# Output projections as seven half-block products in a planned attention kernel

## The chip, the core and the metric

The kernel runs on one core of one Trainium2 chip. The metric is the device time of one execution in microseconds, the median of several runs. The core has five engines that run side by side and wait for each other through semaphores: TensorE (PE: matmuls, with its weight loads as PEld), VectorE (DVE), ScalarE (ACT), GpSimd (POOL) and SyncE (SP), from whose queue nearly all transfers start. Each engine works through its own list of instructions in order.

## What is computed

One layer over 4096 rows of 512 numbers (x), with 3202 rows of context, all float32. In short form:

```python
def layer(x, context):                       # x: 4096 x 512, context: 3202 x 512
    q = heads(layernorm(x, g1, beta1) @ Wq.T + bq)          # 8 heads of 64
    k, v = (heads(layernorm(context, g1, beta1) @ W.T + b) for W, b in ((Wk, bk), (Wv, bv)))
    attn = softmax(q @ k.T / sqrt(64)) @ v
    x1 = x + attn.reshape(4096, 512) @ W_o.T + b_o          # the output projection
    u = (layernorm(x1, g2, beta2) @ W_in.T + b_in) @ Bmat   # 4096 x 64
    s = 0
    for t in range(4096):
        s = silu(s @ A.T) + u[t]
        out[t] = x1[t] + s @ Cmat
    return out + (program_probs.mean(0) @ W_prog.T + b_prog)
```

## The kernel before

**Stages.** A lead of some 186 us turns the context into keys and values and stores them in HBM. Then comes attention: 8 blocks of 512 query rows (`QB`), in each 4 pairs of heads and 2 halves of 256 rows (`QU`), which makes 64 units. A unit walks over the keys in 13 steps of 256. In each step TensorE makes a group of scores (L1095, 16 matmul instructions in 64x64 tiles of the array), ScalarE turns them to weights by an exponential (`weights`, L1172), VectorE adds the weights into the denominators (`add`, L1180), and TensorE multiplies them with the values (`product`, L1229, 16 instructions in 64x64 tiles). The weights live in a ring of `NP` = 15 tiles, from ScalarE's writing until VectorE and TensorE have read them. At the end a unit's output is copied, joined, divided by its denominators (`output`, `join`, `inverse`, `scale`) and kept as a tile of 128 x 256. The scan over the rows is solved by sweeps that mix with the last block and the end, which begins when the last attention product is done.

**Around the units.** Queries of the next block (`queries`): rows are loaded, normalised, turned (`flip` L441, `move` L453) and projected by `by_sevenths`: a product of two matrices, each cut in four quarters, is made from seven products of quarters in place of eight, with sums before and after. `seventh` (L364) is one such product: four matmuls of 128x128 weights by 256 columns. `CHAIN` is the order 1, 2, 6, 5, 7, 3, 4; two banks of PSUM, x and y, take turns, and a product that adds on to a bank waits until the product before it in that bank was read (`before`). Sums of the moving side are made on VectorE (L1468), reads on ScalarE (L1491) and VectorE (L1487).

Output projection (`project`): per half block of 256 rows, two tiles of 128 rows, each by four matmuls of 128x512 (`outs`, L1561); VectorE adds the residual (`x1_`, L1574), which GpSimd has prepared (`row`, L1555); then the second normalisation, `mod` (GpSimd, L1578), the store, the turn, and the product `inputs` (L1618) that gives the scan its input. Blocks 0 to 6 do this for both halves behind the block; of block 7 the first half goes this way and the second through `last_products` (L1881) in the end, beside the last denominators (L1244).

**The order.** `Plan` holds all pieces of the attention stage with engine, cost, dependencies, due date and the rings (`take`, `give`) that they occupy; `order()` runs an event queue over these costs and hands out, engine by engine, the ready piece with the earliest date. The result is the fixed order of instructions. A PE piece of another kind than the last one (64x64 tiles are "quarters", the full array has no kind) costs `ENTER` or `LEAVE` more; pieces of the full array are held together by `KEEP` and `ALONE`. `SHIFT` moves the dates of sorts of pieces by steps of 2150 ns. Loads of keys and values are no pieces: each group of scores issues those of 10 and 6 steps ahead (`load_k` L392, `load_v` L400) on SP's queue when its turn comes.

Of the kernel before, what the change touches and what calls it, by code (L numbers as in the profile page):

```python
# [20 lines left out]
P = 128  # L21
# [20 lines left out]
NP = 15  # L42
NA = 3
# [28 lines left out]
class Plan:  # L72
# [8 lines left out]
    ENTER, LEAVE = 110, 147  # L81
# [3 lines left out]
    PORT = ("add", "rest", "fold", "gather", "scale", "t", "tq", "tied", "wk", "wv", "wq", "rowv")  # L85

    SHIFT = {
        "row.store": 11.5, "fold": 2, "rows.outs": 0.75, "heads": -12, "sample": -3, "spread": 4.75,
        "query.flip": -11, "states": -5.5, "inverse": 4.75, "extra": 10, "scale": -57.75, "rest": -1,
        "row.mod": -17, "joined0": -14.25, "b": -15, "add.l": -23, "l.stats": -34.75, "last": -4.5,  # L90
        "base": -34.75, "inverse.l": -27, "rows.inputs": 3.5, "maximum": -13.5, "fall": -19, "query.stats": -8,
        "den": 4.5, "row.scaled": 12, "l.h": -7, "row.stats": -9.25,
    }

    def __init__(self, rings, held):
# [4 lines left out]
    def add(self, name, engine, cost, run, after=(), due=0, take=(), give=(), kind=None):  # L100
# [4 lines left out]
        elif sort in self.UNIT and name[1] >= self.ENDS:  # L105
# [4 lines left out]
            give=give, kind=kind, at=len(self.pieces),  # L110
# [4 lines left out]
    def order(self):  # L115
# [26 lines left out]
        while len(out) < len(pieces):  # L142
            for e in self.LATE:
# [24 lines left out]
                free[e] = now + cost  # L168
                if shares(p):
                    port = free[e]  # L170
                heapq.heappush(events, (free[e], 0, p["at"], p))
                heapq.heappush(events, (free[e] + self.LATE[e], 1, p["at"], p))
# [5 lines left out]
            while events and events[0][0] <= now:  # L178
                _, late, _, p = heapq.heappop(events)
                if late:  # L180
# [12 lines left out]
def xattn_ssm_kernel(  # L193
# [886 lines left out]

    def parts_of(t):
# [3 lines left out]
    o_t = {}  # L1085
# [194 lines left out]
    def finish(w, i, d, plan):  # L1280
# [33 lines left out]
        plan.add(("output", i), "ACT", 360, partial(output, w), [("product", i, NDC - 1)], d, ["o_"])  # L1314
# [6 lines left out]
        else:  # L1321
            plan.add(("fold", i), "DVE", 680, partial(fold, w), [("add", i, NDC - 1)], d + 500)
            plan.add(("swap", i), "ACT", 760, partial(swap, w), [("fold", i)], d + 600, ["rd"])
            plan.add(("gather", i), "DVE", 860, partial(gather, w), [("swap", i)], d + 700, [],
                     [("rd", ("swap", i))])
            plan.add(("sums", i), "PE", 300, partial(sums, w), [("gather", i), from_(d + 8 * STEP)], d + 1000,
                     ["m", "m"], acc, "quarters")
            opened = ("den", i, 0)
            for k in range(2):
                plan.add(("den", i, k), "ACT", 450, partial(denominators, k),  # L1330
# [19 lines left out]
    def norm_pieces(plan, ks, gets, d, after, names, gives, wait):  # L1350
# [21 lines left out]
        for t, (k, v) in enumerate(zip(ks, vs)):  # L1372
            plan.add((*k, "stats"), "DVE", 870, partial(stats_, v, gets[t], names[t]),
                     [after[t]] + ([(*ks[0], "stats")] if t else []),
# [7 lines left out]
    def queries(plan, Q, d):  # L1382

        copied, w = [], {}
        of_xn = ("query", Q, 0, "move0")
        for half in range(2):
# [4 lines left out]
            def load(t, v=v, at=at):  # L1391
                if t == 0:
                    v["x"] = xp_.tile([P, 2, H], F32, tag="x", name=f"x_{at[0]}")
# [21 lines left out]
            for t in range(2):  # L1415
                plan.add((*ks[t], "flip"), "DVE", 720,
# [7 lines left out]
            d += 2 * QSTEP  # L1424
# [4 lines left out]
    def query_weights(plan, after, d):  # L1429
# [11 lines left out]
        for i, (k, x, y, op) in enumerate(sums):  # L1441
            first = {"6": "5", "7": "6", "3": "7"}.get(k)
            plan.add(("sq", k), "POOL", 1300, partial(sum_, k, x, y, op),
                     [("sq", first)] if first else after, d + i * STEP)

# [6 lines left out]
    def by_sevenths(plan, Q, w, copied, d, of_xn):  # L1452
# [53 lines left out]
        for at, k in enumerate(CHAIN):  # L1506
# [7 lines left out]
            plan.add(("sevenths.read", Q, k), on, 950 if on == "ACT" else 690, partial(read, k), [(*key, k)], d + at, [], gives)  # L1514
# [23 lines left out]

    def project(plan, Q, halves, d, index):

        for half in halves:
# [3 lines left out]
            last = Q == NQB - 1  # L1545
            now = plan.ALONE if last else 0

            def load(t, vs=vs, w=w, at=at):
                if t == 0:
                    w["x"] = xp_.tile([P, 2, H], F32, tag="x", name=f"xr_{at[0]}")  # L1550
# [33 lines left out]
            for t in range(2):  # L1584
# [3 lines left out]
                         [(*ks[t], "load")] + ([] if last else [from_(d - 2 * STEP)]), d - STEP)  # L1588
            plan.add((*k2, "outs"), "PE", 7200, outs,
                     [("scale", i, 0) for i in units_] + [(*k, "row") for k in ks], d - now,  # L1590
                     ["m", "m", "x1"], [("o_", ("output", i)) for i in units_])
            for t in range(2):
# [4 lines left out]
                             [f"y{r}" for r in at], [("x1", (*k2, "outs"))] * 2 * last,  # L1597
                             [] if last else [from_(d + 18 * STEP)])
            for t in range(2):
                plan.add((*ks[t], "mod"), "POOL", 1280, partial(mod, vs[t]), [(*ks[t], "x1")], d + 2 * STEP,  # L1600
                         [], [("x1", (*k2, "outs"))] * last)
                plan.add((*ks[t], "store"), "SP", 800, partial(store, vs[t], at[t]),
                         [(*ks[t], "mod" if last else "flip")], d + 3 * STEP, [], [("x", (*ks[0], "load"))])
# [10 lines left out]
            def inputs(w=w, at=at, last=last):  # L1614
                w["pu"] = m_tile([P, P], f"pu_{at[0]}")
                for c in range(NC):
                    for t in range(2):
                        nc.tensor.matmul(  # L1618
                            w["pu"][t * NS : (t + 1) * NS], wc[:, c, :],
                            w["xn"][:, t, c, :] if last else mixed(w["xn"][:, c, :], t),  # L1620
# [3 lines left out]
            def kept(t, w=w, at=at):  # L1624
                to, c0 = divmod(at[t] // L, NCK)
                hs, of = slice(to * NS, (to + 1) * NS), slice(t * NS, (t + 1) * NS)
                nc.scalar.activation(
                    u[hs, :, c0 : c0 + P // L].rearrange("s j c -> s c j"),
                    w["pu"][of].rearrange("s (c j) -> s c j", j=L),
                    AF.Identity,  # L1630
                    bias=bu2[of],
                    scale=2.0,
                )

            if last:
                plan.add((*k2, "turn"), "PE", 1050, turn, [(*k, "scaled") for k in ks], d + 5 * STEP - now,
                         ["m", "m", "xn2"], [("xh", (*ks[0], "scaled"))])
                for t in range(2):
                    plan.add((*ks[t], "copy"), "ACT", 560, partial(copy, t),
                             [(*k2, "turn")] + ([(*ks[0], "copy")] if t else []), d + 6 * STEP + t, [],  # L1640
                             [("m", (*k2, "turn"))])
                copied, xn2, after = [(*k, "copy") for k in ks], (*k2, "turn"), 7
            else:
                copied, xn2, after = [], (*ks[0], "move0"), 16

                def move_(a, w=w, at=at):
                    if a == 0:
                        w["xn"] = xp_.tile([P, NC, QU], F32, tag="xn2", name=f"xn2_{at[0]}", bufs=1)
                    move(w["xn"], w["x1"], a)

                for t in range(2):
                    plan.add((*ks[t], "flip"), "DVE", 720, lambda t=t, w=w, nv=nv: flip(w["x1"], nv[t]["xh"], t),
                             [(*k, of) for k in ks for of in ("scaled", "mod")], d + 5 * STEP + t, [],
                             [("xh", (*ks[0], "scaled"))])
                for a in range(P // TB):
                    plan.add((*ks[0], f"move{a}"), "SP", 2600, partial(move_, a),
                             [(*k, "flip") for k in ks] + ([xn2] if a else []), d + (6 + 2 * a) * STEP,
                             [] if a else ["xn2"], [("x1", (*k2, "outs"))])
# [796 lines left out]
```

## Time and profile before

| | us |
|---|---|
| median of 3 runs | 1912.04 (1910.61 to 1912.35) |
| the profiled execution | 1913.58 |
| its span, first to last instruction | 1911.7 |
| mean granted TensorE clock | 0.998 |
| lead, up to the first scores of attention | some 186 |
| end, after the last attention product | 55.13 |

The profile is of one execution. It names engines PE, PEld, DVE, ACT, POOL and SP; L12 is line 12 of the kernel. A row of the timeline gives the start in us, the duration, the engine, the line and operation, what is written from what, and how many instructions it merges; in square brackets stands how long the engine was idle before it, and who released it. A row of a group gives "busy us, mean ns of one | idle time before, by releaser". A row of waits gives who waited for whom: the total in us, how often, the longest. A row of a stretch gives its length and the busy time and instructions of each engine. Matmul instructions are pipelined, so their durations overlap: what one costs is read from the distance of starts. A float32 matmul of the program is two matmul instructions.

### The profile page before, as it was taken

How to read it: one execution, taken by the hardware profiler on the slowest of the kernel's cores; microseconds unless marked ns; L12 is line 12 of the kernel's file. 1: busy time of each engine (PE TensorE's matmuls, PEld its weight loads, DVE VectorE, ACT ScalarE, POOL GpSimd, SP SyncE). 2: the span in 40 equal slices, each digit the busy share in tenths (PEclk: the TensorE clock that was granted, in tenths of full speed). 3: DMA queues.
4: the chain of work that ended last, by engine and by line, in shares of the span. 5: the costliest groups of instructions: out<-in, count | busy, mean ns of one | idle time of the engine just before them, and what ended most of it. 6: DMA issues, size and time to landing. Idle time of an engine off the chain costs nothing.

```text
span 1911.7 us, 68126 instructions
## 1 busy us (share of the span) xinstructions
PE 1895.2 (99%) x29464; PEld 1352.6 (71%) x29464; DVE 1535.3 (80%) x2084; ACT 1176.6 (62%) x1675; POOL 237.7 (12%) x382
## 2 busy tenths in 40 slices
PE   9999999999999999999999999999999999999997
PEld 5887679766677667766777667766776677766675
DVE  6642699788879889788878887888978887988876
ACT  3242677576666666656757665766756775756653
POOL 6120000001100120011000120012001110011105
PEclk9999999999999999999999999999999999999999
DMA  7554233132422343224413242234322341544577
GB/s 254 156 158 123 63 102 88 45 101 77 110 71 84 92 126 93 81 75 112 110 41 93 81 121 75 82 89 122 101 68 75 96 122 46 160 120 133 175 197 224
DMA packets 260764, 207.50 MB, mean 109 GB/s; under 512 B 94632, under 2 KB 233896, under 8 KB 260460
## 3 DMA queue, kind: packets, MB, share of 16 engines
q1 hardware_dynamic: 256440, 196.48, 36.6%
q10 hardware_dynamic: 4020, 6.62, 1.1%
q8 instruction: 233, 3.82, 0.9%
q14 instruction: 71, 0.58, 0.1%
HBM read 156.32 MB, written 29.88 MB: 97 GB/s over the span
## 4 chain that ended last, share of the span: by engine, by line


## 5 line engine op out<-in xcount | busy, mean ns | idle before, releaser
L1172 ACT ACTIVATE p<-s,shifts 128x1024 f32<-128x1024 f32 (+1 forms) x832 | 892.9, 1082 | 481.1 <-PE s L1095 464.0
L1180 DVE TENSOR_TENSOR acc<-p,acc 128x1024 f32<-128x1024 f32 (+1 forms) x704 | 829.1, 1178 | 119.8 <-ACT p L1172 85.9
L1095 PE MATMUL s<-q,k 64*64 64x256 f32 x12800 | 837.4, 377 | 0.2 <-ACT p L1172 0.2
L1229 PE MATMUL po<-p,v 64*64 64x256 f32 x12800 | 837.4, 377 | 0.0
L1095 PEld LDWEIGHTS s<-q,k 64*64 64x64 f32 x12800 | 499.9, 133 | 199.5 <-ACT p L1172 16.4
L1229 PEld LDWEIGHTS po<-p,v 64*64 64x64 f32 x12800 | 496.4, 133 | 177.1 <-issue 12.9
L1555 POOL TENSOR_TENSOR xr<-xr,rowb 128x512 f32<-128x512 f32 x30 | 41.3, 1390 | 994.3 <-DMA xr<-in_x_dram 467.4
L1301 DVE RECIPROCAL rd<-rd 128x256 f32<-128x256 f32 (+1 forms) x64 | 110.2, 1723 | 23.5 <-ACT rd L1296 23.5
L1561 PE MATMUL pa<-wo,o 128*128 128x512 f32 x240 | 107.0, 599 | 0.0
L1180 DVE TENSOR_TENSOR acc<-p,p 128x1024 f32<-128x1024 f32 x64 | 78.2, 1222 | 10.9 <-ACT p L1172 10.6
L1561 PEld LDWEIGHTS pa<-wo,o 128*128 128x128 f32 x240 | 44.4, 190 | 56.0 <-issue 56.0
L1204 DVE TENSOR_TENSOR acc<-swap,acc 64x256 f32<-64x256 f32 x126 | 56.7, 450 | 8.9 <-ACT swap L1199 7.0
L1166 DVE TENSOR_TENSOR acc<-x,acc 2x256 f32<-2x256 f32 x128 | 55.0, 430 | 2.5
L1199 ACT COPY swap<-acc 64x256 f32<-64x256 f32 x126 | 50.8, 403 | 6.5 <-DVE acc L1187 3.4
L1578 POOL TENSOR_TENSOR xr<-x,modb 128x512 f32<-128x512 f32 x30 | 38.2, 1273 | 116.9 <-DVE x L1574 116.9
L1491 ACT ACTIVATE q<-qx,bias 128x256 f32<-128x256 f32 x42 | 17.6, 471 | 45.8 <-PE qx L364 45.8
L542 DVE TENSOR_TENSOR ks<-pky,ks 128x512 f32<-128x512 f32 x15 | 10.4, 692 | 43.6 <-PE pky L364 28.7
L1362 POOL TENSOR_SCALAR rstd_x<-mv_x 128x1 f32<-128x1 f32 x28 | 6.2, 221 | 313.5 <-DVE mv_x L1359 311.8
L536 ACT ACTIVATE ks<-pkx,bias 128x256 f32<-128x256 f32 x40 | 16.8, 471 | 45.0 <-PE pkx L364 33.6
L1187 DVE TENSOR_TENSOR acc<-acc 128x512 f32<-128x512 f32 x63 | 43.2, 686 | 1.4
L1278 DVE TENSOR_TENSOR o<-po,o 128x256 f32<-128x256 f32 x64 | 27.0, 421 | 12.3 <-ACT o L1274 7.6
L1129 DVE TENSOR_REDUCE m<-sm 128x1 f32<-128x256 f32 x64 | 24.1, 419 | 15.7 <-PE sm L1115 15.2
(283 smaller groups left out, 1588.8 us busy)
## 6 DMA issues: line engine op xcount, KB each, us to landing
k<-kd SPq DMA_DIRECT2D x432, 128.0 KB, 2.4
v<-vd SPq DMA_DIRECT2D x432, 128.0 KB, 2.3
xn<-x SPq DMA_DIRECT2D x448, 32.0 KB, 1.9
xr<-in_x_dram SPq DMA_DIRECT2D x30, 256.0 KB, 3.4
x1d<-xr SPq DMA_DIRECT2D x30, 256.0 KB, 2.5
x<-in_x_dram SPq DMA_DIRECT2D x28, 256.0 KB, 4.0
cx<-in_ctx_dram SPq DMA_DIRECT2D x25, 256.0 KB, 4.3
kd<-ks SPq DMA_DIRECT2D x20, 256.0 KB, 2.3
```

Source lines behind the costliest of these rows:

```text
L1095: nc.tensor.matmul(s[k0 : k0 + HD, a, b, :], kts[(*w["at"][:2], c)][r, b * CK + k0 : b * CK + k0 + HD], q[r], start=True, stop=True, skip_ ...
L1166: nc.vector.tensor_tensor(to[r], t[r], to[r], ALU.add)
L1172: nc.scalar.activation(t[:, :, :nb, :], w["ps"][c][:, :, :nb, :], AF.Exp, bias=w["shift"])
L1180: nc.vector.tensor_tensor(w["acc"][:, :, :nb, :], t[:, :, :nb, :], before[:, :, :nb, :], ALU.add)
L1187: nc.vector.tensor_tensor(acc[:, :, 0, :], acc[:, :, 0, :], acc[:, :, 1, :], ALU.add)
L1199: nc.scalar.copy(w["swap"][r], of[(1 - k) * HD : (2 - k) * HD])
L1204: nc.vector.tensor_tensor(of[r], w["swap"][r], of[r], ALU.add)
L1229: nc.tensor.matmul(w["po"][k][a * HD : (a + 1) * HD, :QU], vts[Q, hp, c][r, b, a * HD : (a + 1) * HD], t[r, a, b, :], start=(c == 0 and b ...
L1301: nc.vector.reciprocal(w["rd"][:, part], (w["pd"] if last else w["rd"])[:, part])
L1555: nc.gpsimd.tensor_tensor(v["x"], v["x"], rowb, ALU.add)
L1561: nc.tensor.matmul(v["pa"], o_t[Q, c, half][:, t * P : (t + 1) * P], wo[:, c, :], start=(c == 0), stop=(c == NC - 1),)
L1578: nc.gpsimd.tensor_tensor(v["x"], v["x1"], modb, ALU.add)
```

## The change

Blocks 0 to 6 project both halves together, by `project_by_sevenths`: the 512 x 512 output of attention and the 512 x 512 weights are cut in quarters and seven products of quarters replace the sixteen (2 halves x 2 tiles x 4) matmuls of 128x512. The sums of the weights' quarters are made once on GpSimd (`output_weights`), those of the other side per block on VectorE (`so`), and seven reads on VectorE add the products and the residual into the rows (`outs.read`). A unit's outputs are kept in pairs of heads so that a quarter lies in one tile. The later steps of a row move unchanged into `rows_pieces`; the second half's are due 18 steps after the first's.

Tiles: four more of 128x1024 (`alt`), paid by the ring of weights, 15 to 11 (`NP`); `NA` = 7 of these tiles take rows in the end where 3 did. Rows of x have a third tile.

Planner: VectorE's and ScalarE's pieces over 200 ns free the engine 80 and 100 ns before they are done (`OVER`); `ENTER` and `LEAVE` grow; costs of several pieces are set anew; scores are charged 500 ns on SP for each load that they issue (`also`); the first half of the queries is due 13 steps earlier (`EARLY`); `SHIFT` is new throughout.

```diff
-NP = 15
-NA = 3
+NP = 11
+NA = 7
+HALF = 18
+EARLY = 13
+LOAD = 500
+OUTS = 0
...
+    OVER = {"DVE": 80, "ACT": 100}
-    ENTER, LEAVE = 110, 147
+    ENTER, LEAVE = 200, 280
...
-    PORT = ("add", "rest", "fold", "gather", "scale", "t", "tq", "tied", "wk", "wv", "wq", "rowv")
+    PORT = ("add", "rest", "fold", "gather", "scale", "t", "tq", "so", "tied", "wk", "wv", "wq", "rowv")
...
     SHIFT = {
-        "row.store": 11.5, "fold": 2, "rows.outs": 0.75, "heads": -12, "sample": -3, "spread": 4.75,
...
+        "row.store": -0.5, "fold": 5, "rows.outs": 12.25, "heads": -12, "spread": 5.75, "query.flip": -11,
...
-                free[e] = now + cost
+                free[e] = now + cost - (self.over.get(e, 0) if cost > 200 else 0)
+                if p["also"]:
+                    free["SP"] = max(free["SP"], now) + p["also"]
...
+        x_tiles.append(name)
+        if len(x_tiles) % 3 == 1:
+            return alt_tile(6, name)
+        return xp_.tile([P, 2, H], F32, tag="x", name=name)
...
-        o = o_t[Q, hp, half] = op.tile([P, QU], F32, tag="o", name=f"o_{w['name']}", bufs=12)
+        if hp % 2 == 0:
+            t = op.tile([P, 2, QU], F32, tag="o", name=f"o_{w['name']}", bufs=6)
+            for k in range(2):
+                o_t[Q, hp + k, half] = t[:, k]
+            o_pairs[Q, hp // 2, half] = t
+        o = o_t[Q, hp, half]
...
+    def output_weights(plan, after, d):
...
+            nc.gpsimd.tensor_tensor(right[k], x, y, ALU.subtract)
+
+        for i, (k, x, y) in enumerate((("5", b12, b11), ("6", b22, "5"), ("7", b22, b12), ("4", b21, "6"))):
+            plan.add(("to", k), "POOL", 1300, partial(sum_, k, x, y),
+                     [("to", "567"[i - 1])] if i else after, d + i * STEP)
...
+    def project_by_sevenths(plan, Q, d, index):
...
+        def sum_(k):
+            if k == "5":
+                left["5"], left["6"] = parts_of(alt_tile(2, f"so_{Q}"))
+            a11, a12, a21, a22 = v["a"]
+            x, y, op = {
+                "5": (a21, a22, ALU.add), "6": (left["5"], a11, ALU.subtract),
+                "7": (a11, a21, ALU.subtract), "3": (a12, left["6"], ALU.subtract),
+            }[k]
+            nc.vector.tensor_tensor(left[k], x, y, op)
...
+            seventh(v["y" if k in "235" else "x"], left[k], rights[k], k in "125")
+
+        def read(k):
...
+            t = x1s[m][:, :, cs]
+            nc.vector.tensor_tensor(t, of, xs[m][:, :, cs] if k in "1654" else t, ALU.add)
...
+        before = {"6": "1", "5": "2", "7": "6", "3": "5", "4": "7"}
...
+        for at, k in enumerate(CHAIN):
+            after = needs.get(k, [("so", Q, k)]) + ([("outs.read", Q, before[k])] if k in before else [])
+            plan.add((*key, k), "PE", 1740, partial(product_, k), after + last_scale,
+                     d + STEP * 3 // 4 + at - (plan.ALONE if at > 1 else 0),
+                     ["m", "m"] if k == "1" else [], gives[k])
+            plan.add(("outs.read", Q, k), "DVE", 690, partial(read, k), [(*key, k)], d + at,
+                     {"1": ["x1"], "5": ["x1b"]}.get(k, []), [("m", (*key, "1"))] if k in "34" else [])
...
-            plan.add(("weights", i, c), "ACT", 200 + 861 * part, partial(weights, w, c),
+                     [("q", of_q)], "quarters", LOAD * loads)
+            plan.add(("weights", i, c), "ACT", 286 + 828 * part, partial(weights, w, c),
...
-                plan.add(("add", i, c), "DVE", 120 + 1120 * part, partial(add, w, c),
+                plan.add(("add", i, c), "DVE", 135 + 1090 * part, partial(add, w, c),
...
-                s=2, m=2, mt=1, o=1, p=NP, acc=3, extra=4, q=3, tq=1, x=2, x1=1, xn2=1, fs=4,
-                xn=1, xh=2, max=2, rd=2, o_=12,
+                s=2, m=2, mt=1, o=1, p=NP, acc=3, extra=4, q=3, tq=1, x=3, x1=1, xn2=1, fs=4,
+                xn=1, xh=2, max=2, rd=2, o_=6, x1b=1,
...
+        output_weights(plan, [from_(24 * STEP)], 24 * STEP)
...
-                project(plan, Q, range(2), d + 4 * STEP, index)
+                project_by_sevenths(plan, Q, d + (4 + OUTS) * STEP, index)
```

In the order that results, TensorE has 196 matmuls of 128x256 where it had 112 of 128x512, VectorE 49 instructions of 128x512 more and GpSimd 4; the instructions of ScalarE and the transfers are as many as before.

More of the change, by code (lines that the diff above doesn't have):

```diff
@@ L98, in __init__, with add @@
         self.pieces, self.givers = {}, {}
-    def add(self, name, engine, cost, run, after=(), due=0, take=(), give=(), kind=None):
+    def add(self, name, engine, cost, run, after=(), due=0, take=(), give=(), kind=None, also=0):
         assert name not in self.pieces, name
@@ L1513, in by_sevenths @@
             on = READS[k][1]
[L1514 removed]
+            plan.add(("sevenths.read", Q, k), on, 850 if on == "ACT" else 690, partial(read, k), [(*key, k)], d + at, [], gives)
     def mixed(of, t):
@@ L1635, in project @@
[L1635 to L1658, printed above, removed]
-                    copied.append((*ks[0], f"move{a}"))
@@ L2072, in unit @@
             d = (s0 + c) * STEP
+            loads = sum(
+                g < len(steps) and (units[steps[g][0]][2] == 0 or units[steps[g][0]][0] == NQB - 1)
+                for g in (s0 + c + AHEAD_K, s0 + c + AHEAD)
+            )
             g = s0 + c - NDC + AHEAD
```

223 lines of the change are left out of this document (178 added, 45 removed).

## The prediction

> **What bounds the kernel now.** I read the page's totals first, then the busy times by stretch, then who made TensorE wait, then TensorE's timeline at the places that the change rewrites.
>
> ```profile
> span 1911.7 us, 68126 instructions
> PE 1895.2 (99%) x29464; PEld 1352.6 (71%) x29464; DVE 1535.3 (80%) x2084; ACT 1176.6 (62%) x1675; POOL 237.7 (12%) x382
> ```
>
> ```profile
> core 0: us, PE busy (x) PEld busy (x) DVE busy (x) ACT busy (x) POOL busy (x), PEclk, DMA share, GB/s
> 186.00:1856.57 1670.57, 1667.89 (x28128) 1181.84 (x28125) 1403.95 (x1801) 1095.82 (x1505) 164.47 (x242) 1.00 0.35 97
> 427.84:636.31 208.47, 208.47 (x3517) 145.14 (x3513) 177.00 (x228) 137.19 (x189) 21.85 (x32) 1.00 0.33 90
> 1856.57:1911.70 55.13, 43.67 (x504) 27.79 (x502) 36.93 (x102) 16.19 (x54) 24.57 (x31) 0.94 0.75 229
> ```
>
> ```profile
> PE qy L364 <- DVE q L1487: 1.2, 1, 1.2
> PE pu L1618 <- DMA xn<-x: 0.9, 1, 0.9
> PE s L1095 <- ACT p L1172: 0.2, 1, 0.2
> PE sm L1137 <- DVE m L1130: 0.2, 1, 0.2
> ```
>
> The attention stretch, 186 to 1856.57 us, is 87% of the span, and TensorE is busy in all but 2.68 us of it. One block of 512 rows (427.84 to 636.31, from one first output projection to the next) is 208.47 us without a gap. The last four rows are all of TensorE's waits in that stretch: 2.5 us. The granted clock is 1.00. So a microsecond of TensorE work taken out shows in full, unless another engine makes TensorE wait; VectorE comes next, with 177.00 of 208.47 us.
>
> **The change part by part.** *The output products.* What one projection of 256 rows takes, with its two changes between 64x64 tiles and the full array:
>
> ```profile
> 426.00 1.04 PE L1095 MATMUL s<-q,k 64*64 64x256 f32 x16
> 426.87 1.04 PE L1229 MATMUL po<-p,v 64*64 64x256 f32 x16
> 427.84 7.13 PE L1561 MATMUL pa<-wo,o 128*128 128x512 f32 x16
> 434.90 1.09 PE L1095 MATMUL s<-q,k 64*64 64x256 f32 x16
> 435.82 1.04 PE L1229 MATMUL po<-p,v 64*64 64x256 f32 x16
> ```
>
> Durations overlap, so I go by starts. An undisturbed group of scores takes 426.87 - 426.00 = 0.87 (0.865 over several). From 426.87 to 435.82 are 8.95 us for one group of products, the projection and one group of scores: 8.95 - 2 x 0.865 = 7.22 us. A block has two: 14.44 us.
>
> The seven products that replace them exist already in the same form (full array, four matmuls of 128x256, float32) in the query projections:
>
> ```profile
> 545.64 1.91 PE L1095 MATMUL s<-q,k 64*64 64x256 f32 x32
> 547.47 1.99 PE L364 MATMUL qx<-xn,wq 128*128 128x256 f32 x8
> 549.30 1.89 PE L364 MATMUL qy<-xn,wq 128*128 128x256 f32 x8
> 551.03 1.89 PE L364 MATMUL qx<-tq,sq 128*128 128x256 f32 x8
> 552.85 1.09 PE L1229 MATMUL po<-p,v 64*64 64x256 f32 x16
> 553.87 1.99 PE L364 MATMUL qy<-tq,sq 128*128 128x256 f32 x8
> 555.71 1.89 PE L364 MATMUL qx<-xn,sq 128*128 128x256 f32 x8
> 557.43 1.89 PE L364 MATMUL qy<-xn,sq 128*128 128x256 f32 x8
> 559.16 1.89 PE L364 MATMUL qx<-xn,wq 128*128 128x256 f32 x8
> 560.98 1.09 PE L1229 MATMUL po<-p,v 64*64 64x256 f32 x16
> 561.89 1.04 PE L1095 MATMUL s<-q,k 64*64 64x256 f32 x16
> ```
>
> From 545.64 to 561.89 are 16.25 us. They hold four groups of attention (32 + 16 + 16 matmul instructions, 4 x 0.865 = 3.46) and seven products in two runs: 12.79 us. Inside a run a product takes 557.43 - 555.71 = 1.725 us, seven of them 12.08; the rest, 0.71, is two entries and exits, 0.36 us a run. The changed kernel's order on TensorE puts the output products 1 and 2 together, then one group of scores, then 6, 5, 7, 3 and 4: again two runs, 12.79 us. A block gains 14.44 - 12.79 = 1.65 us, seven blocks 11.55 us. In the seventh block the order has three runs (3 and 4 apart): 0.36 back.
>
> *The query products.* Their work stays, but in the changed order all seven stand in one run where before there were two (1, 2, 6 and 5, 7, 3, 4). That is one entry and exit fewer in seven blocks: 7 x 0.36 = 2.5 us. Together: 11.55 - 0.36 + 2.5 = 13.7 us less TensorE work.
>
> The narrow form pays only if its weight loads stay hidden:
>
> ```profile
> L364 PEld LDWEIGHTS qx<-tq,sq x56: 190/190/190, 342.3 to 1596.0; 128*128 128x128 f32 x56
> ```
>
> One load takes 190 ns, and the instructions start 1.725 / 8 = 216 ns apart; in the wide form (7.22 - 0.36) / 16 = 429 ns. So half the columns cost half the time, with 26 ns to spare.
>
> The Trainium skill, "TensorE: Matmul & The Clock Gate", section "Back-to-back issue gap", speaks against that: it says that weight loads share in the spacing of a stream, and gives about 131 ns at 512 columns and 81 at 128. I estimate from that page 98 ns at 256, three quarters of the wide one; by that ratio 56 narrow instructions would replace 32 wide ones at a loss of 56 x 0.75 x 429 - 32 x 429 = 4.3 us a block, 30 us in all. The trace does not follow it for this form.
>
> *VectorE.* Per block four left-hand sums and seven reads replace four residual adds, all 128x512:
>
> ```profile
> L1574 DVE TENSOR_TENSOR x<-pa,xr 128x512 f32<-128x512 f32 x30 | 20.7, 689 | 19.5 <-PE pa L1561 12.9 <-POOL rstd_y L1363 4.2 <-POOL nm_y L1364 1.8
> L1468 DVE TENSOR_TENSOR tq<-xn 128x512 f32<-128x512 f32 x7 | 4.8, 687 | 4.5 <-DMA xn<-x 4.5
> L1172 ACT ACTIVATE p<-s,shifts 128x1024 f32<-128x1024 f32 (+1 forms) x832 | 892.9, 1082 | 481.1 <-PE s L1095 464.0 <-PE sm L1137 5.5 <-PE pd L1257 1.4
> L1555 POOL TENSOR_TENSOR xr<-xr,rowb 128x512 f32<-128x512 f32 x30 | 41.3, 1390 | 994.3 <-DMA xr<-in_x_dram 467.4 <-DMA k<-kd 314.0 <-ACT swap L1199 104.2
> ```
>
> Seven more at 0.69 make 4.8 us a block: 181.8 of about 206.5 us, 88%. It lies beside the products, so I cost it at nothing. What can go wrong is its place: product 6 waits for read 1, 5 for 2, 7 for 6, 3 for 5 and 4 for 7. How long such a link takes is seen in the query run:
>
> ```profile
> 555.91 0.84 ACT L1491 ACTIVATE q<-qy,bias 128x256 f32<-128x256 f32 x2 [2.11 <-PE qy L364]
> 557.70 0.69 DVE L1487 SCALAR_TENSOR_TENSOR q<-qx,q 128x512 f32<-128x512 f32 x1 [1.89 <-PE qx L364]
> ```
>
> A read starts 0.27 us after the next product (557.70 against 557.43) and ends at 558.39; the product that needs it starts at 559.16. The margin is 0.77 us. In the changed order on VectorE one add of weights stands ahead of each of the reads 6, 5, 7 and 3. An add holds the queue like this:
>
> ```profile
> 1852.02 1.23 DVE L1180 TENSOR_TENSOR acc<-p,acc 128x1024 f32<-128x1024 f32 x1 [0.48 <-ACT p L1172]
> 1853.16 1.75 DVE L1301 RECIPROCAL rd<-rd 128x256 f32<-128x256 f32 x1
> ```
>
> If such an add (1.14 us from its start to the next instruction's) began just as its product ended, the read would be 1.14 - 0.77 = 0.37 us late; three such links a block (7, 3, 4) would be 1.1 us, 7.8 us over seven blocks. That is the upper bound; the lower is nothing, since I can follow the queue: after product 2 VectorE has read 2 and add 7 to do, about 1.8 us, beside product 6 of 1.725, and from there adds and products alternate at 0.69 + 1.14 = 1.83 against 1.725 us, so the add begins before its product ends. I take nothing.
>
> *GpSimd* forms four sums of the output weights once: 4 x 1.39 = 5.6 us, in an engine idle for most of the span and planned for the first block, well ahead of the first use near 427.8; nothing, and even uncovered only 5.6.
>
> *Fewer weight buffers, 15 to 11.* The ACT row lists what weights wait for: 464.0 of 481.1 us for scores, and VectorE giving a buffer back is not among the causes. In the new TensorE order scores run at most 7 groups ahead of the products, as before. Nothing; if the cover failed, scores would wait one add, 1.14 us, each time.
>
> *Loads and SP.* The number of transfers is the same; only their places in SP's queue move (query rows 13 steps earlier, a third tile for rows). TensorE waited for a DMA once in the stretch, 0.9 us. Zero, between a gain of 0.9 and a loss of one such wait a block, 6.3. *All other dates* can at best remove the 2.5 us of waits.
>
> *The end.* The changed order puts the last denominators ahead of the last output projection and the first transpose ahead of a scan step; the work is the same.
>
> ```profile
> 1860.20 1.08 PE L1244 MATMUL pd_last<-acc,ones 128*64 128x256 f32 x8
> 1868.36 0.43 PE L1728 MATMUL z<-scan,a_t 64*64 64x128 f32 x4 [1.21 <-DVE scan L1763]
> 1870.40 0.70 PE L1920 MATMUL py_o<-ident,xh_yl 128*128 128x128 f32 x4 [0.93 <-DVE xh_yl L1914]
> ```
>
> These two waits, 2.1 us, are what a better order could win; a worse one could lose as much. I take zero.
>
> *The sum.* The profiled execution took 1913.58 us (span 1911.7 and 1.9 around it); less 13.7 is 1899.9. It lies 1.5 above the median of the runs, 1912.04; measured from that, 1898.4 us. A block should go from 208.47 to 208.47 - 1.65 - 0.36 = 206.46 us.
>
> **The rivals.** *Links break a little* (chance 0.18). The bound above is partly paid, 3 to 8 us: 1901.4 to 1906.4. For it: VectorE at 88%, and the one wait of 1.2 us for a read of query products in the old trace. Against it: that wait came once in fourteen runs.
>
> *Slower* (0.04). That wait of 1.2 us returns in every run of seven, since nothing stands between its products any more: seven query and seven output blocks, 14 x 1.2 = 16.8 us more than the gain of 13.7, 1915.1 us. It decides from 13.7 / 14 = 0.98 us a block and kind. Against it: margins of 0.77 us, and the four products that already ran back to back without a gap.
>
> *Narrow products cost more* (0.01). Were every weight load out in the open, a block's 56 would add 56 x 0.19 = 10.6 us, nine more than it gains: 7 x 9 - 2.2, about 1973 us. Against it: 49 query products of this form, all at 216 ns.
>
> *The gain is given back* (0.03). After seven products in a row, 12.4 us, only two groups of scores have been turned to weights, and TensorE runs dry for the time won: 1908 to 1916, no difference. Against it: after the old run the row of 560.98 follows at once, and five groups of weights lie ready.
>
> *More than counted* (0.09). The new dates also remove the 2.5 us of waits and some of the 2.1 at the end: 1894 to 1896.
>
> **How the numbers follow.** The forecast, 1896.5 to 1901, has 0.65. The range takes in the gain at the end on one side and most of the broken links on the other: 1895 to 1905, leaving out about 0.17. No change is within 0.2%, 3.8 us, about what can be told here: faster needs 1908.2. Faster 0.92 (forecast, more, links), same 0.03, slower 0.05.
>
> **What would show it.** Right: a block period near 206.5 us; seven output products 12.8 us in two runs, 1.725 us each inside; query products as one run of seven; TensorE's waits in the stretch under 3 us in all; the time after the last attention product 54 to 56 us. Wrong: waits of output products for reads or sums on VectorE over 0.5 us each; weights waiting for VectorE's adds; a gap after the run of seven; products at more than 1.8 us.

## The result, and the profile after

The changed kernel takes 1931.03 us (median of 4 runs, 1926.26 to 1933.58) against 1911.99 for the kernel before (1910.61 to 1912.35): ratio 1.0100, 95% interval 1.0087 to 1.0113. It is slower by 19 us, where 13.7 us less were forecast. The profiled execution, the slowest of the four, took 1933.58 us. The head of its page, the stages of before by the same view (attention stage, one block from first output product to first output product, end), and the first row of who made TensorE wait (us in total, times, longest):

```profile
span 1931.7 us, 68735 instructions
```

```profile
186.00:1869.60 1683.60, 1666.58 (x28296) 1230.07 (x28293) 1428.74 (x1852) 1095.16 (x1505) 196.52 (x246) 1.00 0.34 97
435.06:646.38 211.32, 208.99 (x3539) 155.21 (x3536) 180.42 (x235) 137.05 (x189) 24.60 (x32) 0.99 0.32 89
1869.60:1931.70 62.10, 46.43 (x504) 28.56 (x502) 36.47 (x101) 15.58 (x54) 24.83 (x31) 0.88 0.60 192
```

```profile
PE po L1256 <- DVE o L1310: 14.7, 8, 2.5
```

The attention stage has grown from 1670.57 to 1683.60 us, and TensorE now stands idle in it for 17 us where it did for 2.7. One row carries this: eight times the first product of a unit waits for L1310, the *join*, VectorE's sum of the two product banks, which gives the banks back. The end has grown from 55.13 to 62.10 us, at a granted clock of 0.88 for 0.94.

The part that was forecast did come. TensorE's timeline at an output projection and at a run of query products:

```profile
435.06 1.99 PE L382 MATMUL pax<-wo,o 128*128 128x256 f32 x8
...
438.71 1.09 PE L1122 MATMUL s<-q,k 64*64 64x256 f32 x16
439.73 1.99 PE L382 MATMUL pax<-to,so 128*128 128x256 f32 x8
...
443.29 1.89 PE L382 MATMUL pax<-to,o 128*128 128x256 f32 x8
445.02 1.89 PE L382 MATMUL pay<-wo,o 128*128 128x256 f32 x8
...
763.06 1.99 PE L382 MATMUL qx<-xn,wq 128*128 128x256 f32 x8
...
773.52 1.89 PE L382 MATMUL qx<-xn,wq 128*128 128x256 f32 x8
775.34 1.96 PE L1256 MATMUL po<-p,v 64*64 64x256 f32 x32
```

Two runs, 443.29 to 445.02 is 1.73 us inside a run, no link waits for a read, and the query products stand in one run. So the loss lies elsewhere. One of the eight places where a join is late, on VectorE, ScalarE, GpSimd and TensorE of the changed kernel:

```profile
814.57 2.68 DVE L1231 TENSOR_TENSOR acc<-swap,acc 64x256 f32<-64x256 f32 x2 [1.07 <-ACT swap L1226]
817.28 1.23 DVE L1207 TENSOR_TENSOR acc<-p,p 128x1024 f32<-128x1024 f32 x1
818.54 2.79 DVE L1193 TENSOR_TENSOR acc<-x,acc 2x256 f32<-2x256 f32 x2
821.36 1.75 DVE L1333 RECIPROCAL rd<-rd 128x256 f32<-128x256 f32 x1
823.03 0.36 DVE L1310 TENSOR_TENSOR o<-po,o 128x256 f32<-128x256 f32 x1
...
818.94 0.36 ACT L1306 COPY o<-po 128x256 f32<-128x256 f32 x1
...
814.27 2.69 POOL L1608 TENSOR_TENSOR xr<-xr,rowb 128x512 f32<-128x512 f32 x2 [104.45 <-DMA k<-kd]
817.34 3.71 POOL L1608 TENSOR_TENSOR xr<-xr,rowb 128x512 f32<-128x512 f32 x2 [0.38 <-DMA xr<-in_x_dram]
...
820.01 0.61 PE L1142 MATMUL sm<-q,kx 64*64 64x256 f32 x8
820.44 0.59 PE L1256 MATMUL po<-p,v 64*64 64x256 f32 x2
823.45 2.52 PE L1256 MATMUL po<-p,v 64*64 64x256 f32 x27 [2.42 <-DVE o L1310]
```

ScalarE's copy, for which the join waits, ends at 819.30. The join starts at 823.03, 3.73 us later: ahead of it in VectorE's queue stand the two *rest* adds (L1193), 2.79 us for both, and a reciprocal of 1.75. Further ahead stands the *gather* (L1231), 2.68 us for two adds. Beside the gather and the rest adds GpSimd runs four row sums (bias added to rows of x), two beside each. The same place in the kernel before:

```profile
812.80 0.84 DVE L1166 TENSOR_TENSOR acc<-x,acc 2x256 f32<-2x256 f32 x2
813.67 0.43 DVE L1278 TENSOR_TENSOR o<-po,o 128x256 f32<-128x256 f32 x1
...
812.11 0.36 ACT L1274 COPY o<-po 128x256 f32<-128x256 f32 x1
...
807.55 1.27 POOL L1555 TENSOR_TENSOR xr<-xr,rowb 128x512 f32<-128x512 f32 x1 [104.75 <-DMA k<-kd]
809.50 1.28 POOL L1555 TENSOR_TENSOR xr<-xr,rowb 128x512 f32<-128x512 f32 x1 [0.67 <-DMA xr<-in_x_dram]
...
813.23 0.61 PE L1115 MATMUL sm<-q,kx 64*64 64x256 f32 x8
813.84 1.09 PE L1095 MATMUL s<-q,k 64*64 64x256 f32 x16
814.75 2.55 PE L1229 MATMUL po<-p,v 64*64 64x256 f32 x44
```

Three things differ. GpSimd had two sums there, now four, since the planner lets product 1 of the sevenths wait for all four row tiles of the block; the reciprocal has come between rest and join; and TensorE had one more group of scores (813.84) between the unit's end and the next first product. In the changed kernel a wait is the join's lateness less 0.99 us (3.73 gives 2.74, 1.92 gives 0.93). From start to start the six large ones in the blocks are 2.86, 2.65, 2.74, 0.93, 2.51 and 1.91 us, 13.6 in all; one of 1.24 near 227 us and one of 2.43 near 1763 us make it 17.3 (the view of waits counts from the modelled end of a matmul and has 14.7).

A wait also costs clock. Windows of 3.41 us at two of the waits in the changed kernel (us, TensorE busy (instructions), granted clock, DMA share, GB/s):

```profile
820.90:824.31 3.41, 0.99 (x17) 0.99 0.29 105
824.31:827.73 3.42, 3.42 (x39) 0.51 0.00 0
397.56:400.97 3.41, 2.31 (x38) 1.00 0.49 142
400.97:404.38 3.41, 1.97 (x36) 1.00 0.08 31
404.38:407.80 3.42, 3.42 (x68) 1.00 0.02 5
```

The wait of 2.74 us falls into one window, and in the next one TensorE runs at half speed: 39 instructions where an undisturbed window has 68, 1.7 us lost. The longer wait of 2.86 us at 399.5 is split over two windows, and nothing follows. The profile has three such stretches in the attention stage, from 612.6, 824.3 and 1766.3 us: 5.1 us.

### The profile page after: what moved, and what is told of

Its sections match the earlier page's. It is cut to its first block, busy times and chain, and to the rows that moved or that the text cites. A ratio compares the mean times of both kernels' runs of the same rounds, so it can differ in the third digit from the quotient of the medians.

```text
span 1931.7 us, 68735 instructions
## 1 busy us (share of the span) xinstructions
PE 1896.4 (98%) x29632; PEld 1400.8 (73%) x29632; DVE 1559.5 (81%) x2133; ACT 1175.3 (61%) x1675; POOL 269.9 (14%) x386
## 4 chain that ended last, share of the span: by engine, by line
## 5 line engine op out<-in xcount | busy, mean ns | idle before, releaser
L1199 ACT ACTIVATE p<-s,shifts 128x1024 f32<-128x1024 f32 (+1 forms) x832 | 892.3, 1081 | 482.6 <-PE s L1122 466.6
L1256 PE MATMUL po<-p,v 64*64 64x256 f32 x12800 | 916.3, 378 | 14.7 <-DVE o L1310 14.7
L1122 PE MATMUL s<-q,k 64*64 64x256 f32 x12800 | 914.5, 378 | 0.9 <-ACT p L1199 0.9
L1122 PEld LDWEIGHTS s<-q,k 64*64 64x64 f32 x12800 | 547.1, 133 | 193.8 <-ACT p L1199 16.1
L1256 PEld LDWEIGHTS po<-p,v 64*64 64x64 f32 x12800 | 548.5, 133 | 190.3 <-DVE o L1310 21.0
L1395 POOL TENSOR_SCALAR rstd_x<-mv_x 128x1 f32<-128x1 f32 x28 | 16.8, 598 | 377.1 <-DVE mv_x L1392 375.9
L1231 DVE TENSOR_TENSOR acc<-swap,acc 64x256 f32<-64x256 f32 x126 | 58.8, 467 | 11.8 <-ACT swap L1226 10.3
L1193 DVE TENSOR_TENSOR acc<-x,acc 2x256 f32<-2x256 f32 x128 | 66.8, 522 | 1.6
L1310 DVE TENSOR_TENSOR o<-po,o 128x256 f32<-128x256 f32 x64 | 26.4, 413 | 12.8 <-ACT o L1306 11.5
L1328 ACT ACTIVATE rd<-pd 128x128 f32<-128x128 f32 x126 | 33.4, 274 | 1.9 <-PE pd L1284 1.9
L1184 ACT ACTIVATE x<-sm,shifts 128x256 f32<-128x256 f32 x64 | 26.8, 473 | 12.4 <-DVE shifts L1178 12.1
L459 DVE STREAM_TRANSPOSE x<-xh_y 128x512 f32<-128x512 f32 x28 | 18.2, 687 | 18.5 <-ACT xh_y L1403 18.5
```

What stands on the lines that cost most here:

```text
L1122: nc.tensor.matmul(s[k0 : k0 + HD, a, b, :], kts[(*w["at"][:2], c)][r, b * CK + k0 : b * CK + k0 + HD], q[r], start=True, stop=True, skip_ ...
L1193: nc.vector.tensor_tensor(to[r], t[r], to[r], ALU.add)
L1199: nc.scalar.activation(t[:, :, :nb, :], w["ps"][c][:, :, :nb, :], AF.Exp, bias=w["shift"])
L1231: nc.vector.tensor_tensor(of[r], w["swap"][r], of[r], ALU.add)
L1256: nc.tensor.matmul(w["po"][k][a * HD : (a + 1) * HD, :QU], vts[Q, hp, c][r, b, a * HD : (a + 1) * HD], t[r, a, b, :], start=(c == 0 and b ...
L1328: nc.scalar.activation(to, of, AF.Copy, accum_out=rises[:, 3 * i + k : 3 * i + k + 1])
```

## The experiments

Each ratio is to the kernel before, run on the same chip as the experiment (medians 1911.56, 1911.28 and 1910.78 us). What an experiment takes off the loss of 19.0 us is counted against these medians.

**Reciprocal behind the join** (`join_first`). My theory A: the join is late because of what stands ahead of it, rest adds stretched by GpSimd and a reciprocal.

```
+        for p in list(out):
+            if p["name"][0] == "join":
+                at = out.index(p)
+                was = [o for o in out[:at] if o["engine"] == "DVE"][-1]
+                if was["name"][0] == "inverse":
+                    out.remove(was)
+                    out.insert(at, was)
```

> The changed kernel with one order turned round: where a reciprocal of the unit before last stands directly ahead of a join (the sum of the two product banks, after which TensorE may start the next unit's products) on VectorE, the join goes first. Theory A (the join is late because the rest adds, stretched by GpSimd's row sums, and a reciprocal of 1.75 us stand ahead of it; TensorE bears a join that starts 0.99 us after its copy): the six large waits of the changed kernel, 2.86, 2.65, 2.74, 0.93, 2.51 and 1.91 us, fall by 1.75 each to about 3.9 us in all, and the half-speed stretches behind them mostly go: 1916 to 1921 us. Theory B (the reciprocal only fills time in which the join would wait anyway, for VectorE's load with the seven-product sums and reads): waits of TensorE for joins stay above 12 us in all, 1928 us or more.

Measured: 1916.7 us (1915.36 to 1920.74), ratio to the kernel before 1.0031 (1.0020 to 1.0042). The row of waits:

```profile
PE po L1263 <- DVE o L1317: 5.1, 5, 2.1
```

The waits in the blocks are 1.23, 0.86, 0.89, 0.33 and 0.41 us from start to start, 3.7 in all; no half-speed stretch is left in the attention stage. As theory A had it; B has fallen. With the row sums still in place, 13.9 us of the loss are gone.

**Without the row sums** (`no_rows`). The kernel leaves the output bias out of the rows of the seven blocks.

```
         def row(half, t):
-            nc.gpsimd.tensor_tensor(xs[half][:, t], xs[half][:, t], rowb, ALU.add)
+            pass
```

> The changed kernel without GpSimd's four row sums a block (output bias added to the rows of x) in the seven blocks that go by sevenths; that sum is left out of the result. Theory A: the two rest adds ahead of the late join take 0.42 us each again instead of 1.39, the joins come 1.9 us earlier, the six large waits fall to about 3.0 us in all: 1915 to 1920 us. Rival C (GpSimd's sums and the rest adds only happen to lie together, and the reciprocal alone makes the join late): the rest adds get shorter, the waits fall by less than 4 us in all, 1925 us or more.

Measured: 1911.5 us (1909.54 to 1913.53), ratio 1.000 (0.999 to 1.001). The row of waits, then the timeline of VectorE at the same place and the starts of two first output products:

```profile
PE po L1256 <- DVE o L1310: 2.9, 2, 2.0
```

```profile
809.60 0.84 DVE L1193 TENSOR_TENSOR acc<-x,acc 2x256 f32<-2x256 f32 x2
810.47 1.75 DVE L1333 RECIPROCAL rd<-rd 128x256 f32<-128x256 f32 x1
...
432.03 0.70 PE L382 MATMUL pax<-wo,o 128*128 128x256 f32 x2
638.64 0.70 PE L382 MATMUL pax<-wo,o 128*128 128x256 f32 x2
```

The rest adds are back to 0.84 us for both, and the reciprocal, still ahead of the join, does no harm: of the large waits only those at 227 and 1744 us are left. That is better than expected; I had reckoned only the rest adds' 1.9 us, but in the changed kernel the gather ahead of them is stretched by the sums too, so VectorE arrives earlier. The block period is 206.61 us; 206.46 was forecast.

**Both edits** (`both`).

> The two edits together: join ahead of the reciprocal, and no row sums on GpSimd (left out of the result). Theory A: no waits for joins over 0.3 us in the six block places, none of the half-speed stretches in the attention stretch save behind the waits near 228 and 1763 us, which have other causes: 1908 to 1914 us; the block period 206.5 us as forecast. Theory B: 1925 us or more.

Measured: 1911.02 us (1909.15 to 1914.4), ratio 0.9996 (0.9986 to 1.0006). The same as without the row sums alone. So the sums are what it takes: without them the reciprocal costs nothing. But most of the loss needs both, since moving the reciprocal alone already takes 13.9 us away.

**The sevenths with the old dates** (`old_dates_all`). The edit puts the old table `SHIFT` in, `ENTER, LEAVE = 110, 147`, `LOAD = 0`, `EARLY = 0` and `OVER = {}`.

> The seven output products and the smaller rings of the changed kernel, but the planner's dates, costs of entering and leaving, load times, early query rows and early-free engines as in the kernel before. Theory A (the new dates made the loss, by the place of reciprocal and rest ahead of the join; the sevenths are worth what was forecast): 1897 to 1905 us, waits of output products for joins under 2 us in all. Theory B (the sevenths' own extra 4.8 us of VectorE a block are what makes joins late): 1912 us or more, with joins late by 2 us and more in the blocks here too.

Measured: 1962.16 us (1962.11 to 1964.5), ratio 1.0267 (1.0250 to 1.0284). The largest waits of TensorE:

```profile
PE pu L1708 <- DMA xn<-x: 23.3, 8, 4.9
PE po L1249 <- DVE o L1303: 10.8, 7, 2.1
```

My expectation failed. The old dates don't fit the new rows' work (the input products wait 23.3 us for rows to be turned), and TensorE waits for joins here as well; six of the late ones, one a block, have the four row sums beside them. So it is not the new dates alone: the sevenths themselves bring four sums to one place.

**The row sums held back** (`rows_wait`). In the program's order the sums come after the rest adds and the join, but in the changed kernel's trace they start as soon as their rows have landed. One short copy makes them wait:

```
         def row(half, t):
+            if half == 0 and t == 0:
+                nc.gpsimd.tensor_copy(spare, o_t[Q, NC - 1, 1][:, :1])
             ...
```

`spare` is a new tile of one column.

> The changed kernel with all its work and the order of every engine kept; ahead of the four row sums of a block stands one copy of a single column on GpSimd, which reads the tile that the late join writes, so the sums can't start before that join. Theory A (the planner had put the row sums behind the rest adds and the join, but nothing on the chip holds them there, and they start 5 us early, when their rows land; on top of the rest adds they make the join late): the six large waits go as they do without the sums, TensorE's waits for joins are under 4 us in all (those near 228 and 1745 us stay), block period 206.6 us, 1909 to 1914 us. Rival C (what helped without the sums was the GpSimd work saved, not its place): the sums now stretch other VectorE work, waits for joins or scores of over 6 us in all stay, 1920 us or more.

Measured: 1912.19 us (1909.44 to 1915.57), ratio 1.0006 (0.9997 to 1.0016). VectorE and GpSimd at the place (a "x8" row is eight instructions together):

```profile
812.32 0.36 DVE L1311 TENSOR_TENSOR o<-po,o 128x256 f32<-128x256 f32 x1
814.31 13.19 DVE L1208 TENSOR_TENSOR acc<-p,acc 128x1024 f32<-128x1024 f32 x8
...
812.74 0.31 POOL L1610 COPY spare<-o 128x1 f32<-128x1 f32 x1 [110.53 <-DVE o L1311]
813.10 8.01 POOL L1611 TENSOR_TENSOR xr<-xr,rowb 128x512 f32<-128x512 f32 x4
```

The sums start behind the join, the two rest adds (0.84 us) and the reciprocal no longer make it late, and TensorE's waits for joins are 3.0 us, at 227 and 1745 us. All the work is there, and 18.1 us of the loss is gone. The sums still cost VectorE time: eight adds of weights take 13.19 us for 8 x 1.14. But here nobody waits for them.

**Four sums in the kernel before** (`before_rows2`).

```
-                nc.gpsimd.tensor_tensor(v["x"], v["x"], rowb, ALU.add)
+                for _ in range(2 if half == 0 and Q < NQB - 1 else 1):
+                    nc.gpsimd.tensor_tensor(v["x"], v["x"], rowb, ALU.add)
```

> The kernel before, with no sevenths and its old dates, in which GpSimd does the two row sums of the first half of each of seven blocks twice over, so that four stand together as in the changed kernel (the bias is added twice to those rows). Theory A (four sums in a row are enough to make a join late): both rest adds ahead of the join are stretched to 1.4 us where one was, the joins start 2.2 to 2.4 us after their copies (now 1.2 to 1.4), TensorE waits 1.2 to 1.4 us for each of about six: 7 to 9 us, with some half-speed stretches behind them 1918 to 1926 us. Theory B (it takes the sevenths' extra VectorE work, or the reciprocal, as well): under 2 us more, 1914 us or less.

Measured: 1920.13 us (1918.47 to 1920.57), ratio 1.0046 (1.0029 to 1.0062). VectorE and GpSimd:

```profile
811.72 2.60 DVE L1204 TENSOR_TENSOR acc<-swap,acc 64x256 f32<-64x256 f32 x2
814.35 2.19 DVE L1180 TENSOR_TENSOR acc<-p,p 128x1024 f32<-128x1024 f32 x1
...
817.45 0.42 DVE L1278 TENSOR_TENSOR o<-po,o 128x256 f32<-128x256 f32 x1
...
809.73 5.73 POOL L1556 TENSOR_TENSOR xr<-xr,rowb 128x512 f32<-128x512 f32 x4 [105.08 <-DMA k<-kd]
```

The time is as theory A had it, 8.9 us over the kernel before on this chip; the way is not quite. The gather and the first add are stretched, not the rest adds; joins come 2.25 to 3.13 us late at six places, but with a group of scores between, TensorE bears about 2 of that and waits at most 1.1 us at a place. The attention stage grew by 6.5 us. Shown: two more sums there slow a kernel that has neither sevenths nor a reciprocal in the way.

**The last store** (`wait_store`, on top of `rows_wait`).

```
+        names = [p["name"] for p in out]
+        if ("stored1", 15) in names:
+            was = out.pop(names.index(("stored1", 15)))
+            out.insert(names.index(("l.out", 0)), was)
```

> The same, and on the sync queue the store of the last row of the scan goes ahead of the store of the last output rows, where it was last of all. Theory D (that last store costs the end: from the last test of VectorE to the end of the span are 6.8 us in the changed kernel and 3.55 in the kernel before, because the store lands late and the sync engine then waits for a load of instructions): that stretch falls to 3.5 us, the time by 3.0 to 3.4 us against the kernel without this edit. Rival (the end is long for another reason, such as the longer program): under 1 us.

Measured: 1909.76 us (1907.28 to 1912.4), ratio 0.9993 (0.9984 to 1.0003), 2.4 us less than `rows_wait`: less than theory D had, more than the rival. The last transfers of the sync queue and VectorE's last test, in the kernel before and in the changed one:

```profile
1907.36 0.35 SPq L2027 DMA_DIRECT2D out_dram<-xr_l  x1
1907.84 0.14 DVE L2200 TENSOR_SCALAR nbad<-py 1x1 int32<-1x1 f32 x1
```

```profile
1924.10 0.35 SPq L2207 DMA_DIRECT2D out_dram<-xr_l  x1
1924.56 0.37 SPq L2007 DMA_DIRECT2D out_dram<-row  x1
1924.59 0.14 DVE L2384 TENSOR_SCALAR nbad<-py 1x1 int32<-1x1 f32 x1
```

From the reading of that test's flag, 0.33 us after the start of its row, to the end of the span are 3.55 us in the kernel before and 6.79 in the changed one; with the edit 4.75. The stretch differs from program to program: 6.2 to 7.0 us in the changed kernel, `join_first`, `no_rows`, `both` and `rows_wait`, 4.3 to 5.6 in `wait_store`, `best1` and `best2`, which have the edit. So the store explains rather over half; what else the sync queue waits for there the trace doesn't name.

**Three late joins more** (`best1`: `wait_store`, and the same copy ahead of the four sums of output weights and of the last block's row sums).

> The two edits together, and the same one-column copy ahead of the four sums of output weights near 222 us and of the two row sums of the last block near 1745 us. Theory A: the waits of 1.24 and 2.43 us for joins go too, with the half-speed stretch behind the second: 3.7 to 5.4 us less than without these copies, 1901 to 1906 us; TensorE's waits for joins under 0.5 us in all. Rival (those two joins are late for VectorE's other work): less than 1.5 us.

Measured: 1909.22 us (1906.83 to 1910.67), ratio 0.9988 (0.9978 to 0.9998). A miss, 0.5 us less than `wait_store`: the waits for joins are gone, but the delayed sums of output weights make a new wait of 1.7 us near 243 us:

```profile
PE pd L1289 <- ACT x L1189: 1.7, 1, 1.7
```

**The sums of output weights earlier** (`best2`): the copy ahead of them goes, and they stand directly behind the sums of query weights.

```
 ...
+            early = [p for p in out if p["name"][0] == "to"]
+            out = [p for p in out if p["name"][0] != "to"]
+            at = [p["name"] for p in out].index(("sq", "3")) + 1
+            out[at:at] = early
```

> All the work of the changed kernel; the one-column copies hold the row sums behind the late joins of the seven blocks and of the last one, the store of the last row goes ahead of the last output's store, and the four sums of the output weights stand directly behind those of the query weights on GpSimd (near 197 us), where no rest adds run, in place of a copy. Theory A: against the version with a copy ahead of those four sums, the 2.0 us wait that it made near 243 us goes and none comes near 227: 1906 to 1908 us, under 0.5 us of waits for joins. Rival (GpSimd's sums stretch other VectorE work at 197 us and some wait takes their place): 1909 us or more.

Measured: 1906.17 us (1905.2 to 1906.66) against 1910.78 for the kernel before on the same chip, ratio 0.9972 (0.9961 to 0.9984). As expected, the view of waits has none for a join, and this version beats both kernels, the kernel before by 4.6 us. Its attention stage ends at 1846.40 us (1856.57 before).

**Old dates at the end** (`best2_tail`): `best2` without the edit of the store, with the old dates for the last units and the scan.

> The same without the edit of the store, but with the planner's dates of the last stage (last units and scan) as in the kernel before; the planner's order is the same up to that stage. Theory D (the end of the changed kernel is long because its last row is finished and stored late): from the last test of VectorE to the end of the span 3.55 us as before, 2.0 us less than with the store edit alone, and the stage from the last attention product to the end as long as in the kernel before, 55.4 us: 1904 to 1907 us. Rival (the new dates shorten the scan by what the end costs): the stage takes 57 us or more, 1908 us or more.

Measured: 1907.96 us (1907.45 to 1910.51), ratio 0.9982 (0.9973 to 0.9991). A miss: behind VectorE's last test are 4.45 us, not 3.55, and from the end of the last attention product to the end 60.3, against 56.9 in `best2`. All of these 3.4 us more can be clock, since 6.8 us more of its scan ran at half speed. The old dates bring the stretch behind the last test down about as far as the edit of the store does (4.31 in `best2`), but not the whole end; which dates suit it stays open.

## Why the prediction was wrong

*Less TensorE work: right.* From start to start, with their entries, the fourteen old half projections took 103.2 us, the seven new blocks take 92.2: 11.0 us where 11.55 less 0.36 were forecast. The query products, one run each, take 4.8 us less; 2.5 were forecast, and 1.2 of the rest is the wait of the old trace. Narrow products hold 1.73 us, the block period without waits for joins (`no_rows`) is 206.61 against 206.46.

*Links from read to product: right.* No output or query product waits for VectorE. The rivals built on these links did not occur, nor did any sign that I had listed for being wrong. The chance of 0.05 for slower stood on other mechanisms; the path that made the kernel slower was in none of my rivals.

*"GpSimd forms four sums of the output weights once ... nothing": the step that failed*, together with *"It lies beside the products, so I cost it at nothing"* for VectorE. I priced GpSimd by its idle time and asked of VectorE only whether the reads come in time. I did not count that the row sums, same in number, now stand four to a place, nor ask which VectorE instructions they run beside and who waits behind those. What I put at nothing cost, in the profiled execution, 13.6 us of waits for joins in the blocks and 3.4 of clock behind two of them. `no_rows` takes the whole 19.0 us away and `rows_wait` 18.1, and `before_rows2` shows that four sums in a row slow the kernel before as well. The four sums of output weights cost a wait of 1.24 us besides, which is gone in `best1` and `best2`.

*"All other dates can at best remove the 2.5 us of waits": wrong in its bound.* New dates can also add. The place of the reciprocal, ahead of the join, made the joins' waits much longer: `join_first`, which turns only that round, takes 13.9 us away. The wait of 2.43 us near 1763 us is beside the two row sums of the last block, which the change leaves as they were. The attention stage without waits for joins and half speed still has some 5 to 6 us more than forecast, in small pieces: 2.3 us are waits of scan products for VectorE (1.4) and of scores for weights (0.9, before 0.2); the rest I did not track down, nor try which date does it.

*Fewer weight buffers: right.* ScalarE's exponentials wait 466.6 us for scores where it was 464.0, and for VectorE once, 0.7 us.

*"The end ... I take zero", bound 2.1: wrong.* It is 7.0 us longer in the profiled execution. 3.2 of it lie behind VectorE's last test; the other 3.7 lie ahead of the last matmul and go with half-speed stretches. From the end of the last attention product to that of the last matmul, kernels with the new dates take 50.3 us without such a stretch (`no_rows`, `both`, `best1`), 51.4 and 52.0 with one (`best2`, `join_first`), 52.7 with two (`rows_wait`, `wait_store`) and 54.1 with three (the changed kernel); the kernel before takes 50.4 with one. What decides how many come was not tested.

*The sum, by the profiled executions* (20.0 us more span): in the attention stage -15.8 for the products, +17.3 waits for joins, +5.1 half speed, +6.4 smaller pieces and the rest, +13.0 in all; +7.0 at the end. Of the forecast's 13.7 us, `best2` realises 4.6 by its medians. By the profiled executions it is 8.4, but that of the kernel before was slower than all its runs and that of `best2` its fastest. In these two, the attention stage is 10.2 us shorter, where 15.8 went for the products, and the end 1.9 longer: the rest is in those small pieces and the end.

## What to carry to other kernels

When a change moves or gathers work on an engine with time to spare, don't ask whether it has room: list what the other engines do beside it, which of those share its path to memory, and which queue stands behind them. Look above all at the instructions that give a resource of the bounding engine back (here a sum of 0.4 us that frees the product banks) and measure how late each may come; and hold work back with a real dependency, since an order that a planner had in mind binds nothing between two queues.

## What the runs showed of the hardware

A VectorE sum of two operands in the on-chip memory and a sum on GpSimd hold each other up: rest adds of 0.42 us took up to 1.5, gathers of 0.43 mostly 1.2 to 1.4, adds of 1.22 up to 2.3, and GpSimd's sums of 1.28 went to 2.3. Beside the same sums VectorE's reductions (0.41 us) and its reciprocals (1.75) kept their time, and so did its adds with an operand from the product banks (0.66 to 0.69 us) beside GpSimd's `mod` sums of the same size. The Trainium skill, "SBUF — State Buffer", section "Who interferes with whom", states both: an instruction of VectorE with two inputs in that memory contends with one of GpSimd that reads it, the order of issue decides which of the two is blocked, and a reduction never contends. The runs agree; I had not drawn on it for the row sums.

The clock is granted by windows of 3.41 us that run on their own: in the attention stages every half-speed stretch is one or two of them long, and those of the changed kernel start whole numbers of windows apart (62 and 276). In the attention stages of the changed kernel, of `both` and of `wait_store`, each window in which TensorE stood idle for 0.60 or more was followed by one at half speed, and none with 0.55 or less. In `rows_wait` one with 0.57 was not, in `old_dates_all` one with 0.58 was. The Trainium skill, "TensorE: Matmul & The Clock Gate", section "What's actually happening", has free-running windows of 3413 ns and a fall to half speed after an idle one; its section "Why this matters for your kernels" warns of gaps beyond about 3 us. Here waits of 2.4 us were enough where they fell into one window, and 2.86 us did nothing where they fell across two. That may be why the changed kernel's runs spread over 7.3 us where those of the kernel before spread over 1.7; this was not tested.
